# Layer 0 of a sparse two-layer graph network with four batches a step, keys and values in separate tables, and queries made in the step

## The chip, the cores and the metric

The kernel runs on one core of a Trainium2 chip. The metric is the device time of one execution in microseconds (us), taken as the median of several runs. Beside it there is one execution recorded by the hardware profiler, with the time of every instruction on each engine: PE (TensorE; PEld is its weight loading), DVE (VectorE), ACT (ScalarE), POOL (GpSimd) and SP (SyncE), and of the DMA queues.

## What is computed

Input x is 8 batches of 2048 nodes with 256 features, adj a 2048 x 2048 matrix, sparse: a node has its own edge and some 8 others, up to 24 in all. Two layers follow each other, each with a residual and a layernorm around it. The reference, cut to what matters:

```python
# layer 0: attention over the neighbours, 4 heads of 64, softmax within each of 8 chunks of 256 nodes
q, k, v = x @ Wq.T + bq, x @ Wk.T + bk, x @ Wv.T + bv
scores = clip(q . k / 8, -10, 10)          # per head, node n against the nodes of chunk j
scores = where(mask == 0, -10.0, scores)   # so non-edges keep a weight of exp(-10)
ctx = sum over chunks of softmax(scores within the chunk) @ v
out = ctx @ Wo.T + bo + x
g = layernorm(out) * gamma + beta
x = layernorm(x + g)
# layer 1: graph attention, 4 heads of 64
Wh = x @ W
e = leaky_relu(s_src[i] + s_dst[j], 0.2)   # edges only; s_src, s_dst are dot products of Wh with a
x = layernorm(x + elu(softmax(e) @ Wh))
```

## The kernel before

Only edges are computed. edge_lists reads adj, takes up to 24 neighbours of each node, sorts the nodes by how many they have and cuts them into 16 tiles of 128 nodes. Tile t has CAPS[t] slots: 24, 14, 13, 12, 11, 11, 10, 10, 9, 9, 8, 8, 7, 7, 6, 5, which is 164 in all. Non-edges of layer 0 enter through a chunk term: each chunk's sum of v times exp(-10), divided by that chunk's softmax sum z.

Layer 0 works on groups of two batches (G = 2). For each group, tables(g, t) makes keys, values and queries of 128 nodes: four transposes of x on PE, matmuls against wkv and wq, the bias added by a transposing matmul (add_bias), copies by ACT. It writes keys and values side by side into kv_d (1024 floats a node) and queries beside x into qx_d (1024 floats a node). The tables of group 0 are made while adj is read; those of a later group are written into the program beside the steps of the group before it.

A layer-0 step (g, t) is one tile of one group. fetch0 gathers the tile's qx rows and, slot by slot, the kv rows of the neighbours: one indirect DMA on POOL's queue for a slot, 128 rows of 4 KB. Two slots make a unit (UNIT = 2) in a ring of 12 units (RING). scores0 multiplies keys by queries on DVE (L464), sums over the head's dimension by eight accumulating transposes on PE (L469) and a matmul with sel (L479). softmax0 clips, exponentiates, sums within chunks and divides (L486 to L507), and transposes z. context0 adds the chunk term (L523), then for each unit multiplies values by weights in place on DVE (L431, in weighted) and sums the slots by accumulating transposes on PE (L438, in summed). A unit is free when its values are summed. shift0 adds beta to the gathered x on POOL. finish0 applies Wo and bias, adds x (L549), normalizes (moments, rsqrt, L553, L555), adds x + beta, normalizes again, writes x1_d, multiplies by W, and leaves a scatter of the rows to wh_d for the next step (late).

Layer 1 works on four batches at a time. fetch1 gathers rows of 1040 floats (two groups with 512 features and 8 logits each), slot by slot, into the same ring. softmax1 adds the logits of both ends (L586) and needs all slots of the tile before it goes on; context1 weighs and sums like context0, with two accumulators; finish1 applies elu and the residual, normalizes, and leaves four scatters of output rows.

The order of the work is the list seq, written out by hand: 32 steps of groups 0 and 1; then 16 times two layer-0 steps of groups 2 and 3 and one layer-1 step of the first four batches; then 16 layer-1 steps of the last four. In each step of the loop the pending scatters come first, then the gathers of the next step, then the work. POOL's queue takes scatters, gathers and shifts in order, so a scatter that waits for its rows holds the gathers behind it. The program's scheduler may still interleave instructions of neighbouring steps on an engine, by what it holds ready first.

PSUM has eight banks in this kernel: tk 2 (tables), mf 1 (finish0, finish1), tf 2 (scores, z, transposes), pr 1 (products), acc 2 (sums).

The lines of scores0 and of weighted that carry most of DVE's and PE's time:

```python
nc.vector.tensor_tensor(prod[:, :, 0:n * W8].rearrange("p j (s w) -> p s j w", w=W8),
                        u[:, :, 0:GF].rearrange("p s (j w) -> p s j w", w=W8), ...  # L464
nc.vector.tensor_tensor(pv, pv, av, op=ALU.mult)                                    # L431
```

Of the kernel before, what the change touches and what calls it, by code (L numbers as in the profile page):

```python
# [17 lines left out]
P = 128  # L18
# [18 lines left out]
G = 2  # L37
UNIT = 2
RING = 12
WW = 520  # L40
# [4 lines left out]
def edge_lists(tc: tile.TileContext, pool, bank, adj, const, ident, rec_d, B, between):  # L45
# [79 lines left out]
    node2 = const.tile([P, 2, NT], I32, name="node2")  # L125
    for k in range(2):
        nc.vector.tensor_scalar(node2[:, k, :], srt[:, :, TOP + 2], 2.0, float(k), op0=ALU.mult, op1=ALU.add)
# [4 lines left out]
    nc.vector.tensor_scalar(valid, vals, 0.0, None, op0=ALU.is_gt)  # L132
    far = pool.tile([P, NT, TOP], F32, name="far")
# [3 lines left out]
    nc.vector.tensor_copy(idx, far)  # L137
    ohcs = const.tile([P, NT, NCH, TOP], BF16, name="ohcs")
# [19 lines left out]
    op = bank("mf", 1)[0:1, 0:1]  # L158
# [3 lines left out]
    return idx, valid, ohcs, node, node2, nodeb, over  # L162
# [3 lines left out]
def sparse_path(ctx: ExitStack, tc: tile.TileContext, keep, x, adj, Wq, bq, Wk, bk, Wv, bv, Wo, bo, gamma, beta, W, a,  # L166
# [6 lines left out]
    NG = B // G  # L173
    GF = G * F
    GH = G * H
# [3 lines left out]
    kv_d = [nc.dram_tensor(f"kv_d{g}", [N, 2 * GF], F32).ap() for g in range(NG)]  # L179
    qx_d = [nc.dram_tensor(f"qx_d{g}", [N, 2 * GF], F32).ap() for g in range(NG)]  # L180

    wh_d = [nc.dram_tensor(f"wh_d{p}", [2 * N, WW], F32).ap() for p in range(NG // 2)]
    x1_d = [nc.dram_tensor(f"x1_d{p}", [N, 2, GF], F32).ap() for p in range(NG // 2)]
# [5 lines left out]

# [9 lines left out]
    hm = const.tile([H * NCH, H, D], F32, name="hm")  # L199
    nc.gpsimd.memset(hm, EMIN)  # L200

    nc.gpsimd.affine_select(out=hm, in_=hm, compare_op=ALU.is_ge, fill=0.0, base=0, pattern=[[-NCH, H], [0, D]],
                            channel_multiplier=1)
    nc.gpsimd.affine_select(out=hm, in_=hm, compare_op=ALU.is_ge, fill=0.0, base=NCH - 1, pattern=[[NCH, H], [0, D]],
                            channel_multiplier=-1)


    def by_part(v):
        return v.rearrange("p (j h d) -> p h j d", h=H, d=DP)

# [6 lines left out]
                            channel_multiplier=-1)  # L217
    biasT = const.tile([P, 3, KC], F32, name="biasT")
# [6 lines left out]
    ps = ctx.enter_context(tc.tile_pool(name="ps", bufs=2, space=bass.MemoryType.PSUM))  # L225

    def bank(tag, bufs=2):

        return ps.tile([P, 512], F32, tag=tag, name=tag, bufs=bufs)

    with tc.tile_pool(name="prep", bufs=2) as prep:
        for dst, w, scale in ((wq, Wq, 0.125), (wkv[:, :, 0:F], Wk, 1.0), (wkv[:, :, F:], Wv, 1.0), (wo, Wo, 1.0)):
            wn = prep.tile([P, KC, F], F32, tag="wn", name="wn")
            nc.scalar.dma_start(wn, w.rearrange("(c p) f -> p c f", p=P))
            pt = bank("mf", 1).rearrange("p (c f) -> p c f", c=KC)
# [19 lines left out]
        pt = bank("mf", 1).rearrange("p (c f) -> p c f", c=KC)  # L255
# [4 lines left out]
        pa = bank("mf", 1)[:, 0:KC * 2 * H].rearrange("p (c e) -> p c e", c=KC)  # L260
# [14 lines left out]

        bvc = prep.tile([P, KC], F32, tag="bvc", name="bvc")
# [3 lines left out]
        pb = bank("mf", 1)[0:1, 0:F]  # L280
# [3 lines left out]
        one = prep.tile([1, 1], F32, tag="one", name="one", bufs=1)  # L284
        nc.gpsimd.memset(one, 1.0)
        pt = bank("mf", 1)[:, 0:3 * KC].rearrange("p (k c) -> p k c", k=3)
        for k in range(3):
            for c in range(KC):
                nc.tensor.matmul(pt[:, k, c:c + 1], bias_r[:, k, c * P:(c + 1) * P], one, start=(k == 0 and c == 0),
                                 stop=(k == 2 and c == KC - 1), skip_group_check=True)  # L290
        nc.scalar.copy(biasT, pt)


    vsum, xts = {}, {}

    def transposed(t, tag, bufs):

        pt = bank(tag, bufs).rearrange("p (c r) -> p c r", r=P)
        for c in range(G * KC):
            nc.tensor.transpose(pt[:, c, :], t[:, c * P:(c + 1) * P], ident)  # L300
        return pt

    def add_bias(dst, k):

        for c in range(KC):
            nc.tensor.matmul(dst[:, c * P:(c + 1) * P], biasT[:, k, c:c + 1].to_broadcast([P, P]), ident,
                             is_transpose=True, start=False, stop=c == KC - 1, skip_group_check=True)

    def load_x(g, t):
        qx = work.tile([P, 2 * GF], F32, tag="qxs", name="qxs")  # L310
        nc.sync.dma_start(qx[:, GF:].rearrange("p (b f) -> p b f", b=G),
                          x[g * G:(g + 1) * G, t * P:(t + 1) * P, :].rearrange("b p f -> p b f"))
        xts[g, t] = qx

    def tables(g, t):
        if t == 0:
            vsum[g] = small.tile([P, G * KC, NT], F32, tag="xs", name="xs")
        qx = xts.pop((g, t))
        pt = transposed(qx[:, GF:], "tk", 2)
        xT = work.tile([P, G * KC, P], F32, tag="xT", name="xT")  # L320
        for c in range(G * KC):
            nc.scalar.activation(xT[:, c, :], pt[:, c, :], AF.Copy, accum_out=vsum[g][:, c, t:t + 1])  # L322
        kvs = work.tile([P, 2 * GF], F32, tag="kvs", name="kvs", bufs=1)
        vk = kvs[:, 0:GF].rearrange("p (j b f) -> p b j f", b=G, j=NJ)
        for b in range(G):
            pm = bank("tk")
# [7 lines left out]
        for b in range(G):  # L334
            qb = q[:, b * F:(b + 1) * F]
            for kc in range(KC):
                nc.tensor.matmul(qb, xT[:, b * KC + kc, :], wq[:, kc, :], start=(b == 0 and kc == 0), stop=False,
                                 skip_group_check=True)
# [19 lines left out]
    def first_tables(t):  # L358
        if t == 0:
            load_x(0, 0)  # L360
# [761 lines left out]
```

## Time and profile before

| | us |
|---|---|
| median of 3 runs | 3118.27 (3117.54 to 3119.71) |
| span of the profiled execution, first to last instruction | 3102.7 |
| time of the profiled execution beside its span | not shown; the median is 15.6 above the span |
| busy: PE, DVE, POOL, ACT | 2198.2, 2184.7, 1673.6, 756.8 |
| first gather of keys and values | 224 |
| last matmul of a table (L328) | before 1150 |
| first scores of group 2 ready (L486) | 1319.8 |
| first logits of the last layer-1 pass (L590) | 2673.8 |

A row of the profile gives the line of the kernel, the engine, the operation, the tiles (out<-in), a count, busy time and mean duration; then how long the engine was idle ahead of it and what ended that. A view of waits gives, for an engine, what waited for what, the sum in us, how often, and the longest. A view by stretches gives busy time of the engines in each stretch. The granted clock is that of PE as a share of full speed. DMA-issuing instructions on SP and ACT are not counted as busy, while POOL's indirect DMAs are.

### The profile page before, as it was taken

The numbers are of one execution on the slowest core, as the hardware profiler recorded it, in microseconds if no ns is written. First come the engines' busy times: TensorE is split into PE (matmuls) and PEld (weight loads), VectorE is DVE, ScalarE is ACT, GpSimd is POOL, SyncE is SP. The second block draws the span as 40 slices with busy tenths as digits, with TensorE's granted clock in tenths as the row PEclk, the third lists the DMA queues.
The fourth block names the chain that finished last, engine by engine and source line by source line (L and its number), as shares of the span: only waits on it lengthen the run. The fifth ranks groups of instructions, "written<-read, shape, count | busy, mean of one in ns | idle before, by whom it ended". The sixth has DMA issues, their size and how long they took to land. (4 is left out here: it accounts for less than half of the span.)

```text
span 3102.7 us, 38815 instructions
## 1 busy us (share of the span) xinstructions
PE 2198.2 (71%) x13006; PEld 1749.5 (56%) x13006; DVE 2184.7 (70%) x4592; ACT 756.8 (24%) x2404; POOL 1673.6 (54%) x1367
## 2 busy tenths in 40 slices
PE   6778888988989985776666666676666566445554
PEld 3446666766667764555555555555555455335453
DVE  5925768655677756577778777777787885568875
ACT  4642223333233321110111222211122222112222
POOL 0064555544555544356755665657556552688872
PEclk8999999999999987777877777878678778667676
DMA  6656777766587864355666666656566661377761
GB/s 215 229 179 229 275 263 270 247 218 208 191 294 248 280 213 164 107 200 180 231 215 207 211 225 210 220 174 233 200 236 215 220 214 64 129 273 259 274 239 57
DMA packets 219492, 660.62 MB, mean 213 GB/s; under 512 B 43687, under 2 KB 61866, under 8 KB 217238
## 3 DMA queue, kind: packets, MB, share of 16 engines
q0 software_dynamic: 162688, 521.98, 49.6%
q1 hardware_dynamic: 52880, 126.11, 11.0%
q10 hardware_dynamic: 3718, 9.97, 1.0%
q8 instruction: 106, 1.74, 0.2%
q14 instruction: 100, 0.82, 0.1%
HBM read 604.31 MB, written 117.96 MB: 233 GB/s over the span
## 5 line engine op out<-in xcount | busy, mean ns | idle before, releaser
L419 POOL DMA_INDIRECT u<-kv_d,idx x656 | 805.9, 1228 | 269.9 <-issue 140.5
L438 PE MATMUL acc<-ident,u 128*128 128x128 f32 x5248 | 694.1, 292 | 103.1 <-DVE u L431 94.9
L438 PEld LDWEIGHTS acc<-ident,u 128*128 128x128 f32 x5248 | 637.9, 152 | 155.0 <-DVE u L431 137.2
L469 PE MATMUL pr<-ident,prod 128*128 128x128 f32 (+1 forms) x2752 | 428.3, 304 | 293.8 <-DVE prod L464 261.7
L464 DVE TENSOR_TENSOR prod<-u,qx 128x1024 f32<-128x1024 f32 (+1 forms) x344 | 400.8, 1173 | 305.9 <-DMA u<-kv_d,idx 183.2
L469 PEld LDWEIGHTS pr<-ident,prod 128*128 128x128 f32 (+1 forms) x2752 | 347.9, 154 | 372.5 <-DVE prod L464 314.0
L419 POOL DMA_INDIRECT u<-wh_d,idx x328 | 421.4, 1285 | 135.2 <-issue 73.2
L431 DVE TENSOR_TENSOR u<-u,al 128x1024 f32<-128x1024 f32 (+1 forms) x344 | 391.4, 1180 | 0.5
L431 DVE TENSOR_TENSOR u<-u,e 128x1024 f32<-128x1024 f32 (+1 forms) x344 | 385.0, 1163 | 0.5
L570 POOL DMA_INDIRECT wh_d<-whs,node x64 | 75.6, 1181 | 551.8 <-ACT whs L569 518.5
L328 PE MATMUL tk<-wkv,xT 128*128 128x512 f32 x512 | 271.1, 641 | 27.5 <-ACT xT L322 27.5
L300 PE MATMUL tf<-ident,o 128*128 128x128 f32 x256 | 66.7, 378 | 204.4 <-ACT o L411 203.9
L566 PE MATMUL mf<-wa,x1T 128*128 128x264 f32 x512 | 193.7, 514 | 8.7 <-ACT x1T L561 6.1
L644 POOL DMA_INDIRECT out_dram<-y,nodeb x128 | 150.9, 1179 | 88.0 <-ACT y L411 52.9
L386 ACT ACTIVATE y<-mv,eps 128x2 f32<-128x2 f32 (+1 forms) x160 | 47.4, 296 | 505.8 <-DVE mv L401 505.5
L300 PEld LDWEIGHTS tf<-ident,o 128*128 128x128 f32 x256 | 37.4, 185 | 228.9 <-ACT o L411 224.1
L450 POOL DMA_INDIRECT qx<-qx_d,node x64 | 88.4, 1381 | 135.8 <-issue 123.6
L486 DVE TENSOR_SCALAR sc<-tf 128x192 f32<-128x192 f32 (+7 forms) x64 | 15.3, 239 | 206.7 <-PE tf L479 206.7
L634 PE MATMUL mf<-ident,hT 128*128 128x128 f32 x256 | 50.6, 330 | 151.4 <-DVE xr L637 148.2
L586 DVE TENSOR_TENSOR z<-u,sd 128x16 f32<-128x16 f32 (+1 forms) x344 | 54.1, 213 | 144.3 <-DMA u<-wh_d,idx 144.1
L545 PE MATMUL mf<-wo,cT 128*128 128x256 f32 x512 | 146.9, 400 | 6.6 <-DVE xr L637 4.7
L566 PEld LDWEIGHTS mf<-wa,x1T 128*128 128x128 f32 x512 | 114.8, 247 | 50.6 <-ACT x1T L561 18.2
(155 smaller groups left out, 3358.4 us busy)
## 6 DMA issues: line engine op xcount, KB each, us to landing
kv_d<-kvs SPq DMA_DIRECT2D x64, 512.0 KB, 4.3
qx_d<-qxs SPq DMA_DIRECT2D x64, 512.0 KB, 5.0
qxs<-in_x_dram SPq DMA_DIRECT2D x64, 256.0 KB, 3.4
x_d<-o SPq DMA_DIRECT2D x64, 256.0 KB, 2.2
xr<-x_d SPq DMA_DIRECT2D x32, 512.0 KB, 6.8
u<-kv_d,idx POOLq DMA_INDIRECT x656, 6.0
at<-in_adj_dram SPq DMA_DIRECT2D x8, 1024.0 KB, 5.4
at<-in_adj_dram ACTq DMA_DIRECT2D x8, 1024.0 KB, 6.0
```

The lines of the kernel that those rows point to most:

```text
L300: nc.tensor.transpose(pt[:, c, :], t[:, c * P:(c + 1) * P], ident)
L328: nc.tensor.matmul(pm, xT[:, b * KC + kc, :], wkv[:, kc, :], start=(kc == 0), stop=False, skip_group_check=True)
L419: nc.gpsimd.indirect_dma_start(out=u[:, k, 0:width], out_offset=None, in_=table, in_offset=bass.IndirectOffsetOnAxis(ap=idx[:, t, s0 + k:s ...
L431: nc.vector.tensor_tensor(pv, pv, av, op=ALU.mult)
L438: nc.tensor.matmul(acc[:, c, :], part[:, k, c * P:(c + 1) * P], ident, is_transpose=True, start=first and k == 0 and c == 0, stop=last and ...
L450: nc.gpsimd.indirect_dma_start(out=qx, out_offset=None, in_=qx_d[g], in_offset=bass.IndirectOffsetOnAxis(ap=node[:, t:t + 1], axis=0))
L464: nc.vector.tensor_tensor(prod[:, :, 0:n * W8].rearrange("p j (s w) -> p s j w", w=W8), u[:, :, 0:GF].rearrange("p s (j w) -> p s j w", w=W8),
L469: nc.tensor.matmul(pr[0:n * W8, k, :], prod[:, j, 0:n * W8], ident, is_transpose=True, start=(j == 0), stop=(j == NJ - 1), skip_group_chec ...
L545: nc.tensor.matmul(po[:, b, :], cT[:, b * KC + kc, :], wo[:, kc, :], start=(b == 0 and kc == 0), stop=False, skip_group_check=True)
L566: nc.tensor.matmul(pw[:, 0:F + 2 * H], xT[:, b * KC + kc, :], wa[:, kc, :], start=(kc == 0), stop=(kc == KC - 1))
L570: late.append(lambda: nc.gpsimd.indirect_dma_start(out=wh_v[g // 2][g % 2 * NT + t], out_offset=bass.IndirectOffsetOnAxis(ap=node2[:, g % ...
L644: nc.gpsimd.indirect_dma_start(out=out_v[t * B + b], out_offset=bass.IndirectOffsetOnAxis(ap=nodeb[:, t, b:b + 1], axis=0), in_=yv[:, b - ...
```

## The change

Layer 0 takes four batches a step (G = 4), so it has 32 steps of double width instead of 64. Keys and values lie in two tables, k_d and v_d, each with 1024 floats a node for four batches; a slot is two gathers, of keys and of values, into different units, and the ring has 8 units instead of 12. Products of keys and queries are written over the keys, so that a unit of keys is free when its scores are summed. The table of queries is gone: fetch_x gathers four batches' x rows (four indirect DMAs of 128 rows of 1 KB), and query transposes them, adds the bias of the output to them and multiplies by wq within the step before. finish0 puts residual and chunk term into the same PSUM sum as Wo: x by transposing matmuls, the chunk term as one matmul a batch with a matrix (vw) that already holds Wo. The first normalization is applied by ACT from PSUM, then two DVE products with gamma and x + beta. The wh rows of four batches are scattered at once. As the 24 slots of tile 0 do not fit into 8 units, layer 1 gathers the logits of that tile by 24 extra indirect DMAs of 64 bytes a row (zd). PSUM's banks are m 3, acc 2, pr 2, sc 1. seq interleaves one layer-0 step of the second four batches with the layer-1 step of the tile before.

The core of the diff:

```diff
-G = 2
+G = 4
 UNIT = 2
-RING = 12
-WW = 520
+RING = 8
+GF = G * 256
+GH = G * H
+WW = GF + GH
...
-    kv_d = [nc.dram_tensor(f"kv_d{g}", [N, 2 * GF], F32).ap() for g in range(NG)]
-    qx_d = [nc.dram_tensor(f"qx_d{g}", [N, 2 * GF], F32).ap() for g in range(NG)]
+    k_d = [nc.dram_tensor(f"k_d{p}", [N, GF], F32).ap() for p in range(NP)]
+    v_d = [nc.dram_tensor(f"v_d{p}", [N, GF], F32).ap() for p in range(NP)]
...
+    BANKS = {"m": 3, "acc": 2, "pr": 2, "sc": 1}
...
     def tables(p, t):
+        xT = work.tile([P, GK, P], F32, tag="xT", name="xT", bufs=1)
...
+        ks = work.tile([P, GF], F32, tag="ks", name="ks", bufs=1)
+        vs = work.tile([P, GF], F32, tag="vs", name="vs", bufs=1)
...
+        nc.sync.dma_start(k_d[p][t * P:(t + 1) * P, :], ks)
+        nc.sync.dma_start(v_d[p][t * P:(t + 1) * P, :], vs)
...
+    def aggregate(units, al, S):
+        accs = [bank("acc").rearrange("p (c r) -> p c r", r=P) for _ in range(2)]
+        for u, s0, n in units:
+            pv = u[:, :, 0:GF].rearrange("p s (e d) -> p s e d", d=D)
+            av = al[:, :, s0:s0 + n].rearrange("p e s -> p s e").unsqueeze(3).to_broadcast([P, n, GH, D])
+            nc.vector.tensor_tensor(pv, pv, av, op=ALU.mult)
+            for k in range(n):
+                s = s0 + k
+                for c in range(GK):
+                    nc.tensor.matmul(accs[c // 4][:, c % 4, :], u[:, k, c * P:(c + 1) * P], ident, is_transpose=True,
+                                     start=s == 0 and c % 4 == 0, stop=s == S - 1, skip_group_check=True)
+        aT = work.tile([P, GK, P], F32, tag="aT", name="aT", bufs=2)
+        for k in range(2):
+            nc.scalar.copy(aT[:, 4 * k:4 * k + 4], accs[k])
+        return aT
...
+    def fetch_x(p, t):
+        xg = work.tile([P, GF], F32, tag="xg", name="xg", bufs=3)
+        for b in range(G):
+            nc.gpsimd.indirect_dma_start(
+                out=xg[:, b * F:(b + 1) * F], out_offset=None, in_=xrows,
+                in_offset=bass.IndirectOffsetOnAxis(ap=nodeb[:, t, p * G + b:p * G + b + 1], axis=0))
+        qs[p, t] = xg
+
+    def fetch0(p, t):
+        got0[p, t] = gather(GF, k_d[p], t), gather(GF, v_d[p], t)
+
+    def query(p, t):
+        xg = qs[p, t]
+        xT = work.tile([P, G, KC, P], F32, tag="xTs", name="xTs", bufs=2)
+        q = work.tile([P, GF], F32, tag="q", name="q", bufs=2)
+        for half in range(2):
+            pt = transposed(xg, half).rearrange("p (b k) r -> p k b r", k=KC)
+            for kc in range(KC):
+                nc.scalar.activation(xT[:, 2 * half:2 * half + 2, kc, :], pt[:, kc], AF.Identity,
+                                     bias=biasT[:, 2, kc:kc + 1])
...
+        qs[p, t] = xg, xT, q
+
+    def shifted(p, t):
+        xg, xT, q = qs[p, t]
+        xv = xg.rearrange("p (b f) -> p b f", b=G)
+        nc.gpsimd.tensor_tensor(xv, xv, beta_r.unsqueeze(1).to_broadcast([P, G, F]), op=ALU.add)
...
     def scores0(p, t):
+        for i in range(0, len(units), 2):
+            some = units[i:i + 2]
...
+                ku = u[:, :, 0:GF]
+                nc.vector.tensor_tensor(ku, ku, q.unsqueeze(1).to_broadcast([P, n, GF]), op=ALU.mult)
...
     def softmax0(p, t):
-            tmp = work.tile([P, hs, S, NCH], F32, tag="tmp", name="tmp", bufs=1)
-            nc.vector.tensor_tensor(tmp, zh.unsqueeze(2).to_broadcast([P, hs, S, NCH]),
...
-        nc.vector.tensor_tensor(al, al, e, op=ALU.mult)
+            nc.vector.tensor_tensor(tmp, tmp, zh.unsqueeze(3).to_broadcast([P, hs, NCH, S]), op=ALU.mult)
+            nc.vector.tensor_reduce(al[:, h:h + hs], tmp.rearrange("p h c s -> p h s c"), axis=AX.X, op=ALU.add)
...
     def finish0(p, t):
+                for kc in range(KC):
+                    nc.tensor.matmul(po[:, k, kc * P:(kc + 1) * P], xT[:, b, kc, :], ident, is_transpose=True,
+                                     start=(k == 0 and kc == 0), stop=False, skip_group_check=True)
+                nc.tensor.matmul(po[:, k, :], zT, vsum[p][:, b, :], start=False,
                                  stop=False, skip_group_check=True)
...
+        normalized(o, lambda b: pos[b // 2][:, b % 2, :], G)
+        nc.vector.tensor_tensor(o, o, gamma_r.unsqueeze(1).to_broadcast([P, G, F]), op=ALU.mult)
+        nc.vector.tensor_tensor(o, o, xg.rearrange("p (b f) -> p b f", b=G), op=ALU.add)
+        normalized(o, lambda b: o[:, b, :], G)
...
     def fetch1(p, t):
+        if CAPS[t] > UNIT * RING:
+            rows = wh_d[p].rearrange("n (a e) -> (n a) e", e=GH)
+            for s in range(CAPS[t]):
+                nc.gpsimd.indirect_dma_start(
+                    out=zd[:, s, :], out_offset=None, in_=rows,
...
+        got1[p, t] = gather(WW, wh_d[p], t)
...
+    seq = [(0, i) for i in range(NT)]
     for t in range(NT):
+        seq += [(0, NT + t)] + [(1, t - 1)] * (t > 0)
+    seq += [(1, NT - 1 + t) for t in range(NT + 1)]
...
         scatters()
...
+            if layer == 0 and i + 1 < NP * NT:
+                fetch_x((i + 1) // NT, (i + 1) % NT)
+            if seq[k + 1] != (0, NT):
+                fetch(k + 1)
         if layer == 0:
+            scores0(p, t)
+            shifted(p, t)
             if i:
                 finish0((i - 1) // NT, (i - 1) % NT)
+            if p + 1 < NP:
+                tables(p + 1, t)
...
+            softmax0(p, t)
+            if i + 1 < NP * NT:
+                query((i + 1) // NT, (i + 1) % NT)
+            context0(p, t)
```

## Prediction

> **What bounds the kernel now.** I read the totals first, then busy time by stage, then what DVE and POOL waited for, then single rows. The totals name no bottleneck:
>
> ```profile
> PE 2198.2 (71%) x13006; PEld 1749.5 (56%) x13006; DVE 2184.7 (70%) x4592; ACT 756.8 (24%) x2404; POOL 1673.6 (54%) x1367
> ```
>
> So I cut the span where the work changes: lists and first tables (to the first key/value gather at 224), layer 0 of the first four batches (to 1320, with the last table matmul before 1150), layer 0 of the other four with layer 1 of the first four (to 2674), layer 1 of the last four. Columns: stretch, length, busy us of PE, PEld, DVE, ACT, POOL (instructions), granted clock, DMA share, GB/s.
>
> ```profile
> 0.00:224.00 224.00, 162.68 (x621) 96.78 (x622) 137.50 (x497) 110.60 (x323) 46.29 (x67) 0.91 0.60 206
> 224.00:801.60 577.60, 506.18 (x2982) 383.62 (x2981) 370.24 (x660) 169.26 (x650) 287.39 (x236) 0.95 0.69 238
> 801.60:1150.00 348.40, 308.95 (x1868) 238.92 (x1868) 255.17 (x434) 101.43 (x392) 189.22 (x153) 0.96 0.75 263
> 1150.00:1319.80 169.80, 112.73 (x644) 92.58 (x644) 97.97 (x209) 31.60 (x103) 67.20 (x59) 0.75 0.39 129
> 1319.80:2674.00 1354.20, 884.51 (x5448) 736.71 (x5448) 1010.16 (x2046) 257.89 (x754) 793.36 (x643) 0.76 0.60 204
> 2674.00:3103.00 429.00, 223.10 (x1444) 200.85 (x1444) 313.65 (x750) 85.99 (x184) 290.19 (x211) 0.71 0.58 202
> ```
>
> Until 1150 PE is busy 88% of the time: PE sets the pace while it has tables to make. From 1150 no engine reaches 70%, yet a two-batch step with 5 to 8 slots still takes 28 to 30 us: there the chain through one step decides. From 1320 DVE is busy 75%, and its waits in that stage say what fills the rest:
>
> ```profile
> DVE z L586 <- DMA u<-wh_d,idx: 117.9, 44, 12.1
> DVE prod L464 <- DMA u<-kv_d,idx: 74.7, 39, 9.0
> DVE sc L486 <- PE tf L479: 62.3, 16, 12.4
> ```
>
> That is 193 of 344 us of DVE idle for gathers that come late, 62 for scores still on PE. In the last stage POOL decides: 200 us from 2700 hold 164.6 us of busy POOL and 117 instructions, with 0.30 us between one gather and the next, 35 us more: full. How dear a gather is hangs on DVE. Here are POOL and DVE in the same 8 us:
>
> ```profile
> 348.65 1.95 POOL L419 DMA_INDIRECT u<-kv_d,idx  x1 [0.30 <-DVE u L431]
> 350.91 1.97 POOL L419 DMA_INDIRECT u<-kv_d,idx  x1 [0.30 <-DVE u L431]
> ```
>
> ```profile
> 343.98 8.03 DVE L431 TENSOR_TENSOR u<-u,al 128x1024 f32<-128x1024 f32 x7
> ```
>
> Under back-to-back products (one each 1.15 us) a gather lasts 1.96 us and the next starts 2.26 us later; with DVE idle (908 to 915) it is 0.99 and 1.30.
>
> [...]
>
> **The change part by part.** The profiled execution spans 3102.7 us and the page gives no time of its own beyond that; the median of the runs is 15.6 us more, and I carry those over.
>
> *DVE.* All 1032 large products (L464 344, L431 688) become 516 of double length. Back to back one costs 1.147 us[...]: **-41**. The first normalization loses L549, L553, L555 (43.5 + 56.7 + 58.2 = 158) and gets two products of 1024 elements in each of 32 steps, 64 x 1.17 = 75; its shift goes to ACT: **-83**. The reciprocal roots run 96 times for 160: 64 x (224+200+181 ns) = **-39**. Softmax of layer 0 loses L507 (15.2)[...]; a strided product (L503, 1476 ns against L497's 956 for 768 elements) becomes contiguous, but the reduction after it strided: **-35**. Logit sums of layer 1 (L586) halve, **-17**; the mask row (L593) is made once, **-6**. [...] Sum about -213, 10% of DVE's 2185.
>
> *PE.* Away: chunk terms from 512 matmuls (109 us) to 128 wider and deeper ones (estimate 40), transposes of z 35 to 9. Added: 256 transposes of gathered x (0.165 each from L300's rows, 42). Residual transposes replace the bias transposes in finish0 one for one. About -53 in all, and some moves: Q (139 + 50 of bias) leaves the tables for the step.
>
> *POOL.* Key/value gathers stay 656 (fewer steps, two tables), layer 1's stay 328. qx gathers (64) become 128 of x, wh scatters 64 become 32, and 48 small gathers of destination logits come: +80 issues of about 1.3 us, +104; shift0's 64 x 1.38 become 32 of about 2.6. The x gathers come ahead of K, V in the queue; query needs them only after softmax0, with scores and finish0 as cover. The shift now stands behind the next step's gathers, but finish0 needs it only after the next scores.
>
> *ACT and SP.* ACT gets 128 x 0.59 of normalization, 128 activations of 256 elements at 0.38, loses half of the small ones: about +80 on 757, never the busiest. SP loses the qx_d writes (64 x 512 KB), POOL's reads there halve: some 50 of 661 MB. DMA was 60 to 75% busy, so I count nothing.
>
> *Stage 1, +10.* The first gather now needs K, V of four batches: a tile costs 2 x (4.46 + 0.76 + 0.70) = 11.8 us of PE (L328, half of L306, L300 by 224, over 20 tiles), 16 make 189, against 173 that PE had done by 224, four tiles ahead of need. +16, less 7 for 8 ring units to clear instead of 12 (1.8 us each). Single buffers for x, xT, K, V can cost 30 more: -10 to +40.
>
> *Stage 2, -100.* Durations on PE from 224 to 1320 sum to 1072 us for 928 us of busy time. With tables for one group of four (182, Q 116 in the step) and the rest as above the sum is 943, that is 817 busy; at the old 85% it takes 965 us for 1096, -131. I keep -100, because PSUM's tag m (three banks) serves tables, queries and finish0, which holds two of them through a normalization. Bounds -170 and +20.
>
> *Stage 3, -85.* DVE's share of the saving, 123 us, is all on the path if nothing else is late. One score wait per slot set instead of two: -31; o and pr waits (27) mostly go: -20. Against it the **ring**: before, 12 units held K with V; now 8 hold K, then V, then layer 1's set, and softmax1 needs its whole set. With a units of V ahead of it only 8-a fit; at 9 to 14 slots (5 to 7 units) two to six must wait until context0 frees units, at 2.6 to 4.5 us per unit, and 6 us to land. I price that at 10 us in nine of 16 steps: +90. Bounds: -230 (POOL as the next limit: 660 issues x 1.55 + 42 = 1065, at 95% full 1120) and +90.
>
> *Stage 4, +45.* The 24 logit gathers (31 us) precede the 24-slot step; I take half. Five steps of 11 to 14 slots held 6 or 7 of 12 units and prefetched 5; with 8 only one or two: 6 us each, +30. Bounds 0 and +90.
>
> Sum: 10 - 100 - 85 + 45 = -130; 3118 - 130 = **2988 us**.
>
> **Rivals.** (1) *Slower: POOL under long products.* A gather that meets a 2.2 us product could wait for all of it, and 8 units leave no store. After 224 us there are about 1320 issues. At 1.24 + 0.30 each plus 42 they fill 2075 of 2880 us; at 1.75 + 0.30, 2748 with the 42, and 92% full they need 2987; with stage 1 and the 16 us around the span **3230 us**. It decides from a mean of about 1.6 us ((2880 x 0.88 - 42) / 1320 - 0.30). For it: 1.96 under products and stage 4 full already. [...] (2) *No gain:* a four-batch chain takes twice a two-batch one; stage 2 then gives -30, stage 3 -15, stage 4 +45: **3118**. The 28 us of a step with 5 slots, with 16 us of DVE, speak against it. (3) *Twice the gain:* the ring is never short, because POOL is behind DVE anyway; stage 3 -170, stage 2 -130, stage 4 +20: **2850**. (4) Tables, gathers and products are really rearranged, so no change for want of effect is out.
>
> **How the numbers follow.** The case of 2988 gets 0.50 (its own range 2900 to 3080), (3) 0.12, (2) 0.07, (1) 0.31. About 0.2% is what a measurement of this kernel can tell from no change. Faster by more: 0.50 + 0.12 less what of the first reaches no gain, and a little of (2), 0.62; within 0.2% 0.05; slower 0.33. Range **2860 to 3230**: it leaves out the better end of (3) and the worse half of (1).
>
> **What would show it.** Right: products at 2.2 us and 516 of them, DVE near 1970 us in all; the second layer-0 pass begins near 1230; sc waits halve; waits of z for wh_d grow past 118; mean gather below 1.5 us. Wrong: a mean gather above 1.6, POOL waiting for PE (units not free) by hundreds of us, or DVE waiting for k_d and v_d longer than for kv_d before (183).

## The result and the profile after

The changed kernel takes 3145.79 us (median of 9 runs, 3135.08 to 3154.67) where the kernel before takes 3118.27 beside it (9 runs, 3103.22 to 3130.78). The ratio is 1.0082 with a 95% interval of 1.0059 to 1.0104: slower by 0.8%, where 2988 us had been forecast. The profiled execution spans 3143.8 us; that of before spans 3102.7. Of all the executions below, two slow ones, one each of e7 and e8 and over 1.5% above the fastest of their kernel, are left out.

The totals of the page after:

```profile
PE 2090.7 (67%) x12742; PEld 1740.1 (55%) x12742; DVE 1995.8 (63%) x3067; ACT 804.6 (26%) x2441; POOL 1937.0 (62%) x1420
```

PE and DVE have 107 and 189 us less to do than before, and the kernel is 41 us longer. No engine is near full. So the time went into waits, and the cut by stage says where. The four stages end at the first clipped scores of layer 0 (lists and first tables), at the first clipped scores of the second four batches, at the first logits of the last layer-1 pass, and with the kernel. First before (stages 2 to 4; the first took 280.3 us), then after; columns as in the prediction (stretch, length, busy us of PE, PEld, DVE, ACT, POOL, clock, DMA share, GB/s).

```profile
280.30:1319.80 1039.50, 879.93 (x5240) 681.00 (x5239) 708.65 (x1289) 286.34 (x1077) 515.77 (x423) 0.92 0.66 228
1319.80:2673.80 1354.00, 884.51 (x5448) 736.71 (x5448) 1009.96 (x2046) 257.89 (x754) 793.23 (x642) 0.76 0.60 204
2673.80:3102.70 428.90, 223.10 (x1444) 200.85 (x1444) 313.85 (x750) 85.99 (x184) 290.32 (x211) 0.71 0.58 202
```

```profile
0.00:291.70 291.70, 219.99 (x892) 130.62 (x892) 166.59 (x510) 138.98 (x490) 99.21 (x109) 0.91 0.57 195
291.70:1341.80 1050.10, 806.28 (x4857) 652.93 (x4858) 615.73 (x727) 290.41 (x979) 590.32 (x420) 0.89 0.56 190
1341.80:2664.80 1323.00, 849.08 (x5554) 755.22 (x5553) 903.92 (x1256) 291.22 (x788) 934.45 (x659) 0.80 0.58 196
2664.80:3143.80 479.00, 215.36 (x1440) 201.32 (x1440) 309.54 (x576) 84.03 (x184) 313.05 (x235) 0.71 0.60 198
```

Stage 1 grew by 11, stage 2 by 11, stage 3 shrank by 31, stage 4 grew by 50: together 41. In stage 2 PE lost 74 us of work and DVE 93, and the stage got longer. That is the surprise. DVE's longest waits in stage 2 before were these:

```profile
DVE sc L486 <- PE tf L479: 145.8, 20, 13.1
DVE prod L464 <- DMA u<-kv_d,idx: 74.6, 23, 9.0
```

After, the waits of DVE and then of PE name the two engines that hold each other:

```profile
DVE u L518 <- ACT q L498: 308.0, 14, 24.0
DVE sc L534 <- PE sc L527: 60.0, 16, 5.1
DVE u L518 <- DMA u<-k_d,idx: 32.1, 12, 11.8
```

```profile
PE acc L456 <- DVE u L452: 187.2, 45, 16.4
```

DVE stands 308 us before key products, in 14 of 16 steps, until ACT has copied the queries; PE stands 187 us before sums, until DVE has weighted the values. One step of the stage, in the timeline of PE and then of DVE, shows the alternation:

```profile
964.60 1.03 PE L578 MATMUL m<-wo,aT 128*128 128x256 f32 x4
975.20 7.58 PE L456 MATMUL acc<-ident,u 128*128 128x128 f32 x48 [9.57 <-DVE u L452]
984.15 1.97 PE L456 MATMUL acc<-ident,u 128*128 128x128 f32 x16 [1.37 <-DVE u L452]
987.73 2.16 PE L319 MATMUL m<-ident,o 128*128 128x128 f32 x8 [1.61 <-ACT o L431]
989.68 5.26 PE L594 MATMUL m<-wa,x1T 128*128 128x264 f32 x16
994.78 1.04 PE L319 MATMUL m<-ident,xl 128*128 128x128 f32 x8
...
1003.80 0.60 PE L319 MATMUL m<-ident,xg 128*128 128x128 f32 x4
```

```profile
986.88 0.16 DVE L429 SCALAR_TENSOR_TENSOR nm<-mv,r 128x4 f32<-128x4 f32 x1
1010.39 2.29 DVE L518 TENSOR_TENSOR u<-u,q 128x2048 f32<-128x2048 f32 x1 [23.35 <-ACT q L498]
```

From 965.6 PE has nothing for 9.57 us, as DVE does softmax0 and the first weighted values. Then it sums them, finishes the step before (L319 with o, L594), makes a table (994.8 to 1003.8) and only then the query (1003.8 to 1009.7). DVE has been done since 987.0 and waits 23.35 us for it. For the transposition of z and the query the trace shows no other wait than their place in PE's queue: z was ready at 969.5, the gathered x a step earlier, and PE stood idle from 965.6 to 975.2.

In the later stages layer 1's waits for gathers grew, from 117.9 us in stage 3 (shown in the prediction) and, in stage 4, from

```profile
DVE z L586 <- DMA u<-wh_d,idx: 26.1, 8, 7.0
```

DVE, stage 3 and stage 4 after:

```profile
DVE z L620 <- DMA u<-wh_d,idx: 170.2, 36, 12.0
DVE z L620 <- DMA zd<-wh_d,idxd: 48.9, 2, 29.9
DVE u L518 <- ACT q L498: 44.6, 4, 14.1
DVE sc L534 <- PE sc L527: 35.4, 13, 7.5
```

```profile
DVE z L620 <- DMA u<-wh_d,idx: 93.1, 36, 6.4
DVE xr L655 <- ACT y L654: 31.8, 10, 8.4
```

Gathers take 1574 ns for keys, 1377 for values and 1350 for layer 1 in the mean; before they took 1228 (keys with values) and 1285 (layer 1).

### The profile page after: what moved, and what is told of

Read it like the earlier page. It is cut to its first block, busy times and chain, and to the rows that moved or that the text cites. A ratio compares the mean times of both kernels' runs of the same rounds, so it can differ in the third digit from the quotient of the medians.

```text
span 3143.8 us, 36386 instructions
## 1 busy us (share of the span) xinstructions
PE 2090.7 (67%) x12742; PEld 1740.1 (55%) x12742; DVE 1995.8 (63%) x3067; ACT 804.6 (26%) x2441; POOL 1937.0 (62%) x1420
## 5 line engine op out<-in xcount | busy, mean ns | idle before, releaser
L439 POOL DMA_INDIRECT u<-k_d,idx x328 | 516.1, 1574 | 289.2 <-PE acc L456 138.8
L518 DVE TENSOR_TENSOR u<-u,q 128x2048 f32<-128x2048 f32 (+1 forms) x172 | 370.4, 2187 | 470.8 <-ACT q L498 352.6
L439 POOL DMA_INDIRECT u<-v_d,idx x328 | 451.8, 1377 | 227.3 <-PE acc L456 83.3
L439 POOL DMA_INDIRECT u<-wh_d,idx x328 | 442.8, 1350 | 181.1 <-PE acc L456 84.8
L521 PE MATMUL pr<-ident,u 128*128 128x128 f32 x2624 | 357.8, 294 | 117.7 <-DVE u L518 104.9
L521 PEld LDWEIGHTS pr<-ident,u 128*128 128x128 f32 x2624 | 321.8, 154 | 148.7 <-DVE u L518 131.0
L452 DVE TENSOR_TENSOR u<-u,e 128x2048 f32<-128x2048 f32 (+1 forms) x172 | 372.4, 2188 | 33.0 <-DMA u<-wh_d,idx 26.1
L452 DVE TENSOR_TENSOR u<-u,al 128x2048 f32<-128x2048 f32 (+1 forms) x172 | 382.3, 2252 | 2.6 <-PE acc L456 2.1
L350 PE MATMUL m<-wkv,xT 128*128 128x512 f32 x512 | 253.5, 619 | 31.2 <-ACT vs L353 26.1
L473 POOL DMA_INDIRECT xg<-in_x_dram,nodeb x128 | 159.7, 1248 | 77.3 <-issue 34.8
L620 DVE TENSOR_TENSOR z<-u,sd 128x32 f32<-128x32 f32 (+1 forms) x148 | 30.0, 225 | 263.3 <-DMA u<-wh_d,idx 263.3
L594 PE MATMUL m<-wa,x1T 128*128 128x264 f32 x512 | 143.6, 440 | 0.3
L319 PE MATMUL m<-ident,o 128*128 128x128 f32 x256 | 61.3, 361 | 119.2 <-ACT o L431 117.9
```

What stands on the lines that cost most here:

```text
L350: nc.tensor.matmul(pm, xT[:, b * KC + kc, :], wkv[:, kc, :], start=(kc == 0), stop=False, skip_group_check=True)
L439: nc.gpsimd.indirect_dma_start(out=u[:, k, 0:width], out_offset=None, in_=table, in_offset=bass.IndirectOffsetOnAxis(ap=idx[:, t, s0 + k:s ...
L473: nc.gpsimd.indirect_dma_start(out=xg[:, b * F:(b + 1) * F], out_offset=None, in_=xrows, in_offset=bass.IndirectOffsetOnAxis(ap=nodeb[:, t ...
L518: nc.vector.tensor_tensor(ku, ku, q.unsqueeze(1).to_broadcast([P, n, GF]), op=ALU.mult)
L521: nc.tensor.matmul(pr[:, s0 + k - first, :], u[:, k, j * P:(j + 1) * P], ident, is_transpose=True, start=(j == 0), stop=(j == NJ - 1), ski ...
L594: nc.tensor.matmul(pw[:, 0:F + 2 * H], xT[:, b * KC + kc, :], wa[:, kc, :], start=(kc == 0), stop=(kc == KC - 1))
```

## The experiments

The runs are named e1 to e15 in the order in which they were made, and fall in four sets, each on one chip. On two of the chips the kernel before took 3123 to 3124 us (e1 to e4, e9 to e12), close to the 3118 above, on the two others 3235 (e5 to e8) and 3206 (e13 to e15). Across sets only ratios to the kernel before on the same chip are compared; the changed kernel stands at 1.0082, and a point is one hundredth of such a ratio. The changed kernel itself was not run on the two slower chips, so there 1.0082 is an assumption. The edits that ran on both of them differ between them by 0.7 points (e5 and e14) and 0.3 (e6 and e15), so a gain counted from 1.0082 on these chips is not known to better than about a point. Lengths of stages are those of one profiled execution.

**The query's place.** Two kernels let the query go earlier. The first gives it a PSUM bank of its own (one of the two banks of pr), so that it does not queue for tag m behind finish0 and tables:

```diff
-    BANKS = {"m": 3, "acc": 2, "pr": 2, "sc": 1}
+    BANKS = {"m": 3, "acc": 2, "pr": 1, "sc": 1, "qb": 1}
-            pt = transposed(xg, half)....
+            pt = transposed(xg, half, "qb")....
-            pq = bank("m")
+            pq = bank("qb")
```

> The changed kernel, with one bank of pr (2 to 1) given to query as a tag of its own, program order unchanged. Theory (order on PE): query shares tag m with finish0, tables and the transpose of z, whose banks are handed out in program order, so PE does it after finish0's tail and the tables, and DVE waits for q (308 us in the first pass of layer 0, 45 in the second). With its own bank PE can do query while context0 runs: the wait for q falls below 80 us, the first pass from 1050 us to 850 to 930, the whole to 2940 to 3030 us. Rival (ring): q is only where the wait shows; with q early DVE waits for k_d instead, because 8 units hold too little; the first pass loses less than 40 us, the whole stays at 3105 or above. Second rival (PE has no room): PE is 77% busy in that pass, one pr bank costs what query gains; the whole 3120 to 3180.

Measured: 3073.03 us, ratio 0.9846 (0.9802 to 0.989). Faster, but by less than expected. The wait for q is gone; in stage 2 its time is now a wait for the scores:

```profile
DVE sc L534 <- PE sc L527: 267.7, 16, 33.1
```

That stage shrank only to 1024.8 us; stage 3, with no tables, gave 49, about the 44.6 us for which it had waited for q. So the query's bank mattered, but in stage 2 what comes behind PE's block of finish0 and table is late, the scores if not the query.

The second calls query between finish0 and tables:

```diff
+            if i + 1 < NP * NT:
+                query((i + 1) // NT, (i + 1) % NT)
             if p + 1 < NP:
                 tables(p + 1, t)
```

> The changed kernel with query called behind finish0 and ahead of the tables, all banks as they were. Theory (order on PE): the tables (about 9 us of PE a step in the first pass) leave the chain that ends in q, finish0's tail stays in it; the wait for q falls from 308 us by 100 to 150 in the first pass and hardly in the second, where there are no tables; the whole to 3000 to 3060 us. Rival (ring): the whole stays at 3105 or above and waits for k_d grow by what q's wait loses. If a step's own length is PE's, tables only move behind and nothing changes.

Measured: 3133.55 us, 1.0029 (1.0015 to 1.0043). The wait for q fell as expected, the total did not. The same exchange: the wait for q in stage 2 is 191.1 instead of 308.0, that for the scores 131.5 instead of 60.0. So it is not the place of the query alone that costs.

**The ring.**

```diff
-RING = 8
+RING = 7
```

> The changed kernel with 7 ring units instead of 8, nothing else. Theory (order on PE sets the first pass, the ring sets the layer-1 passes): the first pass gets longer by less than 15 us; in the last pass, where the waits of z for its gathers are 93 us, the steps of 9 to 14 slots lose about 6 us each, 30 to 60 us in all, and the second pass 30 to 80; the whole 3200 to 3280 us. Rival (the ring sets the first pass too): the first pass alone gets longer by over 40 us. If the ring doesn't matter anywhere: within 15 us of 3146.

Measured: 3154.74 us, 1.0091 (1.0056 to 1.0126), which is not clear of 1.0082. In the trace only stage 4 is longer, 504.2 us for 479.0, with DVE's wait for layer 1's gathers there at 121.2 for 93.1. Stages 2 and 3 are 1042.9 and 1314.4, not longer. So the ring limits the last stage, not layer 0; 25 us there are less than the 30 to 60 expected, and the 30 to 80 expected in stage 3 did not come.

**The length of a product.** Each product of two slots (2048 elements) becomes two of 1024, for keys (L518) and for values (L452):

```diff
-            nc.vector.tensor_tensor(pv, pv, av, op=ALU.mult)
+            for k in range(n):
+                nc.vector.tensor_tensor(pv[:, k:k + 1], pv[:, k:k + 1], av[:, k:k + 1], op=ALU.mult)
```

> The changed kernel with each product of 2048 elements made as two of 1024 (keys by queries, and weights by values or rows), the rest as it is. Theory (long products hold POOL up): gathers fall from a mean of 1.57 (k_d), 1.38 (v_d), 1.35 (wh_d) us to about 1.25, POOL loses 150 us of busy time[...]. If that holding up costs time on the path, the whole falls by 30 to 80 us. If POOL's waits are for free units anyway and not for its own speed: the gathers get shorter all the same, and the whole is within 20 us of 3146[...].

Measured: 3025.64 us, 0.9701 (0.9634 to 0.9767). Stages 277.8, 1008.3, 1242.9, 487.7: 42 us less in stage 2, 80 less in stage 3. That is more than the 30 to 80 us expected, though the gathers hardly got shorter: those of keys have a mean of 1449 ns for 1574, the others no shorter one (1376 and 1380 for 1377 and 1350). This run doesn't say whether shorter gathers or an earlier start of PE brought the gain, so a further kernel keeps the short products and lets PE take the second slot of each unit first (the start and stop flags of the sums follow the new order):

```diff
-            for k in range(n):
+            for k in reversed(range(n)):
                 s = s0 + k
```

> Products of one slot (1024 elements) as in the split kernel, which took 3025.6, but PE takes the second slot of each unit first, so that it starts on a unit only when both products are done, as behind one long product. Theory A (the gain of the split is that PE starts a slot earlier): the gain goes, 3110 to 3150. Theory B (the gain of the split is in shorter gathers, since no product is 2.2 us long): it stays, 3015 to 3050. In between both have a part.

> Products of one slot with PE taking the second slot first, again, beside the kernel before on this chip. At the ratio that it had on the slower chip (0.986): 3070 to 3090. If the whole gain of the split is the earlier start of PE: 3130 to 3150; if none of it: 3015 to 3040.

Measured on two chips: 3189.86 us at 0.9858 (0.9807 to 0.9909), and 3182.88 at 0.989 (0.9831 to 0.995). From 1.0082 to 0.9701 the split gained 3.8 points; with PE late 1.9 to 2.2 of them remain, if 1.0082 holds on these chips. So PE's earlier start has a part in the gain; how large it is, the intervals and the chips leave open. What the rest is stays open too. Shorter gathers are one candidate, though in the mean those of values and layer 1 got no shorter in the split kernel. Another is that finish0's small instructions, which stand between the products on DVE, wait behind 1.2 us instead of 2.3; no run parts the two.

**Was PE the limit of stage 2 before?** The prediction said so. This kernel takes PE's and ACT's work on most later tables away from the kernel *before*:

```diff
+        if g and t:
+            nc.scalar.copy(qx[:, 0:GF], kept[0][:, 0:GF])
+            nc.sync.dma_start(kv_d[g][t * P:(t + 1) * P, :], kept[0])
+            nc.sync.dma_start(qx_d[g][t * P:(t + 1) * P, :], qx)
...
+            return
```

> The kernel before, without PE's and ACT's work on the tables of groups 1 to 3 except the first tile of each: the other tiles' keys, values and queries are copies of the first tile's, with the same transfers. In its second stage 340 us of PE durations belong to tables (1072 us of durations are 880 us busy); about 15 of 16 go, some 260 us of busy PE. Theory A (PE sets the pace of that stage, as the prediction had it): the stage shortens in proportion, from 1040 to 730 to 800 us, and the kernel is 240 to 310 us faster. Theory B (a two-batch step is a chain that takes 28 to 30 us with or without a table, as after the last table): the stage stays at 32 x 28 to 30 = 900 to 960 us, and the kernel is 80 to 140 us faster.

Measured: 3185.32 us, 1.0223 (1.0149 to 1.0296): slower, which neither theory had. Its second stage, as a whole:

```profile
290.20:1395.00 1104.80, 749.55 (x4176) 613.87 (x4174) 705.29 (x1285) 197.98 (x615) 495.89 (x423) 0.74 0.58 205
```

PE's busy time fell from 880 to 750 us and the stage grew from 1039.5 to 1104.8. The instructions that write or read the tables' PSUM banks (tk), before and in this kernel (stretch, length, busy us of PE, PEld, DVE, ACT):

```profile
280.30:1319.80 1039.50, 304.72 (x1132) 169.32 (x1131) 2.02 (x3) 119.51 (x510) 0.92 0.66 228
```

```profile
290.20:1395.00 1104.80, 20.80 (x68) 10.18 (x66) 1.36 (x2) 4.91 (x18) 0.74 0.58 205
```

So some 284 us of PE's table work went. The rest of PE's work, the same 4108 instructions, takes some 154 us longer (879.9 - 304.7 before, 749.6 - 20.8 here), and the granted clock fell from 0.92 to 0.74. The matmuls of finish0 with wa show it, before and in this kernel (its lines are numbered 16 higher):

```profile
L566 PE MATMUL mf<-wa,x1T 128*128 128x264 f32 x248 | 79.1, 447 | 1.4 <-ACT x1T L561 1.3
```

```profile
L582 PE MATMUL mf<-wa,x1T 128*128 128x264 f32 x248 | 105.8, 569 | 9.2 <-ACT whs L585 8.5 <-ACT x1T L577 0.7
```

The run mixes two effects, then: no tables, and slower matmuls. An estimate from these numbers: if nothing else became slower, the slower matmuls can have lengthened the stage by no more than their own 154 us, and it grew by 65, so the tables had cost at most some 90 us of the stage, for 305 us of PE's time. The trace of before points the same way without any edit. Four tiles (11 to 14) of the first group, with tables beside them, and of the second, without (columns as for the stages, from clipped scores to clipped scores):

```profile
640.20:761.60 121.40, 100.18 (x546) 75.34 (x546) 67.65 (x146) 37.51 (x147) 51.71 (x43) 0.92 0.65 219
1162.00:1279.30 117.30, 72.87 (x395) 58.12 (x394) 67.44 (x146) 20.95 (x71) 48.76 (x44) 0.72 0.48 161
```

PE is busy 83% of the time in the one and 62% in the other, again at a lower clock, and the steps take almost the same time. So being 85% busy was not what set the stage; most of the table work filled gaps between the links of a chain. In these runs the clock was lower where PE had less to do, 0.92 and 0.74 with PE busy 85% and 68% of the stage. But the busy share alone does not set it: the changed kernel without its tables, below, has 0.88 at 73%, and stage 3 after 0.80 at 64%.

What the chain of before ran through is less clear. DVE's longest wait in that stage was for scores on PE (145.8 us), the next for gathered keys and values (74.6), both shown above. POOL stood 249.0 us before the scatters of finish0's rows, with the next step's gathers behind them, but that can count only as far as gathers came late. No run cut one of these links in the kernel before.

**Is the table on the path after?** The same work taken away from the changed kernel, for the second four batches:

```diff
+        if p and t:
+            nc.sync.dma_start(k_d[p][t * P:(t + 1) * P, :], kept[0])
+            nc.sync.dma_start(v_d[p][t * P:(t + 1) * P, :], kept[1])
...
+            return
```

> The changed kernel, without PE's and ACT's work on the tables of the second four batches except those of the first tile: the others are copies, with the same transfers. A table takes PE 8.7 us and lies between finish0 and the query on PE in each of 15 steps. If PE's order puts the table on the chain of each step: -130 in the second stage (1050 to 920), total near 3015 where the changed kernel takes 3146. If PE only happens to be there and another chain (gathers, units) sets the step: -0 to -40, total 3105 to 3146.

Measured: 3019.24 us, 0.9671 (0.9623 to 0.9719), as the first theory had it.

```profile
295.40:1214.80 919.40, 672.24 (x4363) 584.84 (x4362) 628.00 (x704) 213.32 (x602) 598.41 (x421) 0.88 0.60 205
```

Stage 2 fell by 131 us with 134 us less of busy PE: one for one, and the clock stayed where it was (0.88 for 0.89). The wait for q fell from 308.0 to 164.2. Table work that had mostly filled gaps before lies on the path after.

**Cutting the ties.** A tie is here a wait of DVE for a result of PE. Key products by constant queries (the tile of q then has one buffer instead of two), softmax0 from constant scores, and both:

```diff
-        q = qs[p, t][2]
+        q = q0
```

```diff
-        nc.vector.tensor_scalar(sc, st0.pop((p, t)).rearrange("p s e -> p e s"), -10.0, ...
+        nc.vector.tensor_scalar(sc, s0c[:, 0:GH * S].rearrange("p (s e) -> p e s", e=GH), -10.0, ...
```

> All key products multiply by the queries of tile 0 instead of the tile's own; the queries are still made in every step, with the same transposes and matmuls, but nothing reads them. Theory A (the query made within the step ties the key products of the next step to PE's queue, which the changed kernel added): the 308 us that the key products wait for q go; 806 us of busy PE at the 85% of the kernel before make the second stage 950 us instead of 1050, and with 45 us of the same wait in the third stage the total is 2990 to 3030. Theory B (four batches a step make the chain longer in itself): DVE then waits for the scores on PE instead, as with the query in its own bank (268 us); the second stage stays at 1010 to 1040 and the total at 3060 to 3110.

> The kernel with key products by the queries of tile 0 again, now on the same chip as the cut of the scores; on a chip where the kernel before took 3235 it stood at 0.966 of that. If the query is the tie that costs: 3000 to 3030, most of the 167 us that both cuts gave. If the two ties cost only together (a wait for q that becomes a wait for scores): 3080 to 3130.

> softmax0 reads a tile of zeros instead of the scores; the queries stay the tile's own. With both cut the kernel took 2978.8, 167 us less than the changed kernel. If the query is the tie that costs, cutting the scores alone gives little: the 308 us wait for q stay in the second stage, total 3090 to 3140. If the scores are the tie, it gives most of the 167: 2980 to 3030.

> Key products multiply by the queries of tile 0 and softmax0 reads a tile of zeros instead of the scores, so that DVE waits for PE in layer 0 only in finish0's normalization and for free units; PE does all its work, and nothing reads its scores and later queries. If the chain from the query through scores and softmax to the values is what makes a step long: the second stage falls from 1050 to the time that PE's 806 us busy need at 88%, 915 to 950 us, and the total to 2960 to 3010 on a chip where the changed kernel takes 3146. If it stays near the 0.966 of the kernel before that the constant query alone gave, units that PE frees late, or finish0, set the step, and not this chain.

| cut | us | ratio to before (95%) | less than 1.0082, points |
|---|---|---|---|
| query (e5) | 3130.48 | 0.9661 (0.9614 to 0.9708) | 4.2 |
| query (e14) | 3121.85 | 0.9732 (0.9712 to 0.9752) | 3.5 |
| scores (e13) | 3076.83 | 0.9585 (0.9553 to 0.9617) | 5.0 |
| both (e11) | 2978.80 | 0.9539 (0.9491 to 0.9586) | 5.4 |

The queries and the scores are two links of one loop: query on PE, key products, scores on PE, softmax0, values, sums on PE, and behind these in PE's queue the next query. Cutting a link moves the wait. With the query constant (e14), DVE in stage 2 waits 128.7 us for scores and 160.1 for gathered keys, and the stage is still 1024.5 us (1032.8 in e5). With the scores constant, DVE waits for no query; between the first key products of the first and of the second four batches it waits instead

```profile
DVE z L551 <- PE m L558: 114.3, 14, 21.2
DVE u L452 <- DMA u<-v_d,idx: 113.6, 55, 12.9
```

the first of these for PE's transposition of an older z. As clipping then no longer waits for scores and cannot mark the stage, it is counted from key products to key products: 1045.4 us in the changed kernel and 937.1 with both ties cut; 1015.6 with the query constant (e14) and 1011.5 with the scores constant, these two on a slower chip. The kernel before has 1030.3. So with both cut the stage is 93 us shorter than before, about the 100 that had been forecast for it. On the one chip that has both single cuts, the scores are the better place to cut, by 1.5 points.

The expectations put the whole gain on one tie or the other. By the ratios neither holds, and the two gains do not add: 3.5 to 4.2 and 5.0 give 5.4. By the microseconds (3145.8 for the changed kernel) they would more than add: 24 and 69 give 167. The single cuts ran on the slower chips, so whether they add depends on carrying ratios from chip to chip, and stays open.

**Putting the gains together.** First the edits of e1 and e4 in one kernel.

> Split products and the query's own PSUM bank together. If the two gains come from different waits they add up: 3146 - 120 - 73 = 2950, 2930 to 2980. If both take away the same wait (DVE and PE waiting for each other within a step), about 3015 to 3040.

Measured: 3101.72 us, 0.9577 (0.9506 to 0.9649). The two gains (2.4 and 3.8 points) give 5.1 of the 6.2 that they would make if they added; with these intervals, and on one of the slower chips, that does not rule out that they add. With the query's bank taken from m instead of pr:

```diff
-    BANKS = {"m": 3, "acc": 2, "pr": 1, "sc": 1, "qb": 1}
+    BANKS = {"m": 2, "acc": 2, "pr": 2, "sc": 1, "qb": 1}
```

> As the one before, but the query's bank is taken from m (2 banks left for tables, finish0, z) and the products keep two banks. If one bank for products is what made DVE wait 268 us for scores in the kernel with the query's own bank, this is 20 to 60 us faster than the one before; if finish0, which holds two m banks through its normalization, then shuts out tables and z, it is 20 to 60 us slower.

Measured: 3079.79 us, 0.9502 (0.9442 to 0.9562). The intervals of the two overlap, so which bank is better given up is not decided. DVE still waits 295.3 us for scores in stage 2, so that wait does not need a single pr bank.

```diff
-RING = 8
+RING = 9
-        wh = work.tile([P, WW], F32, tag="whs", name="whs")
+        wh = work.tile([P, WW], F32, tag="whs", name="whs", bufs=1)
```

> Split products, the query's own bank with m at two, and nine units in the ring instead of eight (the tile of wh rows then has one buffer instead of two). The ring is short in the third and fourth stage only: seven units cost 25 us in the last stage, so nine give back 15 to 25 us there and 10 to 30 in the third; the ratio to the kernel before goes from 0.950 to 0.933 to 0.945. If the single buffer of wh rows holds up finish0, it stays at 0.95 or above.

Measured: 2979.16 us, 0.9545 (0.9499 to 0.9592). By the ratio, on another chip, a ninth unit with one buffer of wh rows shows no gain over e8. In the trace the last stage is shorter, 466.6 us for 487.7 in e4 and 490.5 in e8, as expected, and as one unit fewer had made it longer. Both kernels stand 4 to 6% below the kernel before, keep the whole change, and are the best versions here. Even there DVE waits for scores, in stage 2 of the last one:

```profile
DVE sc L536 <- PE sc L529: 305.3, 16, 27.5
```

## Why the prediction was wrong

**Work: right for DVE and PE, not for POOL.** DVE was to fall by 213 us, it fell by 189. The products take 2187 and 2252 ns where 2.2 us was forecast, 1125 us in all for 1177 before: 52 us less, where the -41 was the author's estimate. Softmax of layer 0 (L486 to L507 before, L534 to L551 after) fell from 349 to 298 us, by 51, where the -35 was in part an estimate. The sum of 213 also counts 8 us of added time, an estimate that no trace showed. PE was to have 817 us of busy work from the first gather to the end of stage 2; from that gather (237.8) to 1341.8 it has some 839. POOL was to gain about 100 us and gained 263: its gathers of keys and values, as many as before, take 968 us for 806, a stretch that the sum had put at nothing and only rival (1) considered.

**Stage 1: right.** +11 for +10.

**Stage 2: here the sign was lost.** Forecast -100, measured +11; the second pass over layer 0 begins at 1341.8 where 1230 was named as the sign. The step that failed is "that is 817 busy; at the old 85% it takes 965". It treated PE's busy share as the stage's limit and carried it over. PE has 806 us busy in the stage after, near the forecast, and the stage takes 1050: 77%, not 85. Nor was PE's share the limit before, where four tiles took 121.4 us with tables and 117.3 without. The working had the evidence in hand: "a two-batch step with 5 to 8 slots still takes 28 to 30 us" without tables, hardly less than the 1039.5 / 32 = 32.5 us of a step of that stage, with more slots and tables.

Rival (2), that "a four-batch chain takes twice a two-batch one", came nearest: 1050.1 / 16 = 65.6 us a step. It was given 0.07, and its -30 was still too good; with the +10 of stage 1 its terms also add up to 3128, not 3118. That it came near does not make the chain the same one doubled: DVE waited for scores and gathers before, and for queries after. What the runs show in place of the failed step is a loop through PE that sets the step after the change: taking 134 us of tables off PE shortens the stage by 131, and cutting both ties by 108. How much the same cuts would give in the kernel before was not tried.

Second failing step, in *POOL*: "query needs them only after softmax0, with scores and finish0 as cover". That speaks of the transfer of x, and the transfer was indeed early. It forgot what stands ahead of the query on PE: sums, finish0's tail and a table, 28.6 us in the step shown (975.2 to 1003.8). "I keep -100, because PSUM's tag m ... serves tables, queries and finish0" named the resource, and priced it at 31 us; the wait for q is 308.

**Stage 3: -85 forecast, -31 measured.** The terms that were written down held: DVE -106 for -123, scores -27 for -31, waits for gathers of layer 1 (L586 before, L620 after with zd) from 117.9 to 219.1, which is +101 for the ring's +90. Missing was the query: 44.6 us of wait for q, the same failing step; a bank of its own for the query took 49 us from this stage. The kernel with seven units speaks against the name "ring" for that +101: one unit fewer did not lengthen this stage. So the size was right, its cause is not shown, and that the size fits may be luck.

**Stage 4: right in size.** +50 for +45. Logits wait 93.1 us for 26.1. One unit fewer adds 25 us and one more takes 21 (e12 beside e4), which supports the ring here. The nearness of the sum is in part luck: the wait for gathers grew by 67, and DVE's wait for y (L637 before, L655 after), which the working did not have, fell from 67.6 to 31.8.

**Rival (1)**, gathers held by long products, had 0.31 by the author's estimate and was to decide from a mean of 1.6 us. Key gathers reach 1.57, the others 1.35 to 1.38. One of its signs did come true: POOL waits 306.9 us for PE to free units. If what remains of the split with PE late is all put down to it, it costs about two points; taking the tables' work away from PE and ACT gives four (1.0082 to 0.9671). Rival (3), a ring that is never short, falls with the waits for layer 1's gathers.

## What to carry to other kernels

An engine that is 85% busy need not be the limit: before pricing its work as time, find a stretch of the same trace without that work, and compare the length of a step and the granted clock. When work is moved into a step, list what stands ahead of it in its engine's order and its PSUM tag, and ask which engine waits behind it; a value that used to be fetched from memory, and is now made within the step, becomes a link of a loop. Doubling the work of a step halves the number of turns, and gains nothing if each turn of the loop doubles too.

## What the hardware showed that was not expected

Taking work from PE cost time: 2.2% (1.5 to 3.0) slower with 37 of some 39 tables of stage 2 gone from PE, at a clock of 0.74 for 0.92, and matmuls of one kind at 569 ns for 447 in the mean. In the changed kernel the tables could go and the clock stayed, 0.88 for 0.89; what makes the difference is not shown.

The stretch of a gather under a product grew with the product. After, beside products of 2.29 us with others of 1.22 between them, and then with DVE soon idle (0.99):

```profile
979.14 2.48 POOL L439 DMA_INDIRECT u<-v_d,idx  x1 [10.61 <-PE acc L456]
981.93 3.03 POOL L439 DMA_INDIRECT u<-v_d,idx  x1 [0.30 <-DVE o L583]
985.26 0.99 POOL L439 DMA_INDIRECT u<-v_d,idx  x1 [0.30 <-DVE st L424]
```

Here the two gathers took 2.48 and 3.03 us. Under products of 1.15 us the longest that the prediction showed was 1.97. What part of a gather is held up is not shown.

The chips differ more than the effect: the kernel before took 3123 to 3235 us on four of them, so ratios to a run on the same chip are needed. Even these need not carry over: the kernel with constant queries has 0.9661 on one chip and 0.9732 on another.
